# k2's projection by Strassen's algorithm, the output projection's first row tile in two groups, weight sums in place

## The chip, the cores and the metric

The kernel runs on one core of a Trainium2 chip, as one launch. Its metric is the device time of an execution in microseconds (us). TensorE (PE) multiplies matrices; VectorE (DVE) and ScalarE (ACT) work on tiles element by element; GpSimd (POOL) and SyncE (SP) here mostly issue DMAs. Each engine runs its instructions in order and waits on semaphores for the others. SBUF is the on-chip memory of 128 partitions; PSUM, in banks of 512 float32 per partition, takes the results of matmuls.

## The reference

A layer of a graph network with a feed-forward block, all in float32. x has N = 384 rows (nodes) of F = 1024 features.

```python
h = layernorm(x)
q, k, v = h @ wq.T + bq, h @ wk.T + bk, h @ wv.T + bv
q2, k2, v2 = q @ wiq.T + biq, k @ wik.T + bik, v @ wiv.T + biv     # then 16 heads of 64
mask = full((N, N), -inf); mask[src, dst] = softplus(w)[type - 1]   # 12288 edges, the last one wins
mask[i, i] = w[3] where it is still -inf
attn = softmax(q2 @ k2.T / 8 + mask)                                # for each head
x = x + (attn @ v2) @ wo.T + bo
y = layernorm(x)
g = silu(y @ w1.T * s1) * (y @ w2.T * s2)
x = x + gelu(gelu(g @ h1.T * t1) @ h2.T * t2) @ w3.T * s3
```

The seven matrices w* of the attention are 1024 x 1024; those of the feed-forward block are ternary.

## The kernel before, in words

**Layout.** Activations are kept transposed, features on partitions in 8 blocks of 128 and the 384 nodes along the row; v2 and the output projection have nodes on partitions, in three row tiles. A weight matrix is loaded as two halves of 512 output columns, 2 MB each, into a pool of four buffers (`load_w`, `prefetch`). `plan` names the halves in the order of their use; a half is asked for when an earlier one is done with. All these loads go through SP's queue; only the feed-forward weights, rounded on the way, go through POOL's.

**Order.** The instructions of SP, ACT, DVE and PE stand in the order in which the program writes them; POOL's are placed by the scheduler, with the DMAs of `load_w` kept in program order. The stages on PE: transposes of the normalised x, q (`project`), q2, v (`project_fast`), v2, k (`project_fast`), then k2 with the attention, the output projection, the feed-forward block (`rest`).

**Strassen's algorithm (Winograd's form).** `project_fast` computes a 1024 x 1024 projection by seven products of half the size. Its operands are sums of quarters of the input (`row_sums`: s1 to s4) and of quarters of the weight (b11 to b22). A product is 16 matmuls of 128 x 128 weights with 192 columns, into two of six PSUM banks; DVE and ACT add the products up. The weight sums are DVE operations on 128 x 2048 elements: `third` writes b22 - b12 into a tile t3 of its own, `first` makes b12 - b11 in place of b12, then b11 += t3 and b21 -= b11 stand between the products (lines 459 to 501). The functions in `beside` are called between the products: chunks of the edge table, weight sums for the next stage, or the bias `xs += bo`. v2 does the same with nodes on partitions, for two of its three row tiles (lines 531 to 571); the third is multiplied directly (`last_tile`).

**The mask.** The 12288 edges, 96 columns of 128, are scattered into a table in DRAM by 96 indirect DMAs on POOL, one column each. Where a cell occurs twice the last edge has to win: `targets` compares, on DVE, each edge with those of the next columns, and sends the earlier ones to a spare cell. `flight` is how many columns may be under way at once: 3 for those groups of 16 columns that `DENSE` lists, else 2. A `chunk` is eight columns. The values and the fill are negated, since the softmax works on -score: `nmask` is read back (line 575, on POOL) once the last scatters have landed, and the k2 projection carries the factor -0.125.

**The attention.** There are 24 units: a pair of heads and a row tile of 128 nodes. They run in 13 slots of mostly two units. In a slot PE multiplies the scores (`scores`, in PSUM tiles of a pool of four), DVE adds the mask and takes the row's extreme (`exponentials`), ACT makes the exponentials and their sums, DVE scales them (`normalised`); in the next slot PE transposes them (`transposed`) and DVE and ACT copy the results to SBUF; when three units of a pair are there, `weighted` multiplies with v2, and ACT adds the bias into aT. Between the two units' transposes PE does matmuls of the k2 projection. `project_k2` is a generator of 64 matmuls, 8 for each of 8 output blocks of 128 features: AHEAD = 3 blocks go ahead of the first slot, the others are shared out over the slots. Its results and the products av take turns in a pool of two PSUM banks. In the last two slots and after them PE begins the output projection (`out_steps`, eight matmuls of 512 columns for a row tile and half). `inspect` reads the feed-forward weights once to see whether they are exact in a short format: SP loads 512 KB, ACT reduces them.

**The end.** `multiply_out` and `add_out` finish the output projection and its sum with x row tile by row tile, each followed by its layernorm; the feed-forward block begins with rows 0 to 255 while row tile 2 is normalised. The last outputs are multiplied, added and stored one after the other.

## Time and profile before

| | |
|---|---|
| Median of three runs | 402.02 us (400.39 to 405.31) |
| Profiled execution | 396.56 us, of which 394.3 us are the profile's span |
| PE busy | 383.2 us (97%) |
| DVE, POOL, ACT busy | 234.1, 129.7, 106.1 us |
| TensorE clock granted | 0.996 |
| DMA | 59.88 MB, mean 152 GB/s |

Stages on PE, by the chain that ended last (us from the span's start): first matmul of q 13.2; q2 54.5 to 92.1; v to 128.6; v2 to 166.4; k to 202.8; k2's first three blocks to 218.3; the slots to about 299.6; the output projection to 340.7; the feed-forward block to 382.2; the last additions to 390.6.

A line of the page names the line of the kernel, the engine and the operation, then the tile written and those read, the shape and the count; behind the bar stand the busy time in us and the mean of one in ns, and then how long the engine had stood idle before these instructions and what ended that. In a timeline each row is a start, a duration, and in brackets an idle time just before it and its releaser. Consecutive instructions on an engine overlap a little, so the distance from start to start is the better price. Waits give a total, how often, and the longest.

### The profile page before, as it was taken

To read this page: it belongs to the slowest core of one execution; us is meant where nothing else is said; L and a number is where in the kernel's file an instruction comes from. 1 tells how busy PE (TensorE), PEld (TensorE's weight loads), DVE (VectorE), ACT (ScalarE), POOL (GpSimd) and SP (SyncE) were. 2 spreads that over 40 slices of the span, in tenths; PEclk is the share of its full clock that TensorE was granted. 3 is DMA by queue.
4 is the path that set the end of the run, shared out by engine and by line. 5 is a ranking of instruction groups with operands and counts; after the bars stand their busy time and mean duration, and the time that the engine had idled before them with its cause. 6 is when DMAs were issued, how large, how long until landed. Compare 5 with 4: busy or idle time off the path is not lost.

```text
span 394.3 us, 4956 instructions
## 1 busy us (share of the span) xinstructions
PE 383.2 (97%) x1829; PEld 277.8 (70%) x1829; DVE 234.1 (59%) x623; ACT 106.1 (27%) x235; POOL 129.7 (33%) x114
## 2 busy tenths in 40 slices
PE   6899999999999999999999999999999999999994
PEld 6555578999999444599985556564645445699983
DVE  5695798974699773653720396767751055222456
ACT  3610010000000010020001287757761386142420
POOL 3024466785686287777742000000000000200000
PEclk9999999999999999999999999999999999999998
DMA  8799998319320920380086281011196040570004
GB/s 284 244 363 310 292 302 303 92 48 378 112 68 19 364 99 0 118 309 2 0 278 256 61 265 57 12 42 53 32 342 216 0 161 0 143 284 0 2 1 163
DMA packets 30250, 59.88 MB, mean 152 GB/s; under 512 B 5424, under 2 KB 8336, under 8 KB 30096
## 3 DMA queue, kind: packets, MB, share of 16 engines
q1 hardware_dynamic: 23056, 50.09, 37.0%
q0 software_dynamic: 6880, 9.03, 7.9%
q10 hardware_dynamic: 288, 0.41, 0.3%
q8 instruction: 16, 0.26, 0.3%
q14 instruction: 10, 0.08, 0.1%
HBM read 57.26 MB, written 2.26 MB: 151 GB/s over the span
## 4 chain that ended last, share of the span: by engine, by line
PE 79%; DVE 11%; DMA 8%; ACT 1%; issue 0%; SPq 0%; DVEq 0%; ACTq 0%
PE ps L454 25%; PE ps L598 11%; PE ps L619 10%; PE ps L538 10%; PE ps L800 6%; DMA wiq<-in_wiq 5%; PE av L676 4%; PE sc L635 4%; PE pp L667 4%; PE ps L812 4%; DVE jk L350 3%; DMA xs<-in_x 1%; DVE y L895 1%; DMA kr<-keyd 1%; DVE y L894 1%; DVE sums L415 1%
## 5 line engine op out<-in xcount | busy, mean ns | idle before, releaser
L366 POOL DMA_INDIRECT tab<-val,cell x96 | 121.3, 1263 | 90.8 <-DMA tab<-val,cell 43.9
L350 DVE SCALAR_TENSOR_TENSOR jk<-kr,key,jp 128x384 bf16<-128x384 f32 (+1 forms) x96 | 48.2, 564 | 5.4 <-DMA kr<-keyd 5.4
L619 PE MATMUL ps<-kT,wik 128*128 128x384 f32 x128 | 43.4, 487 | 0.0
L598 PE MATMUL ps<-wo,aT 128*128 128x512 f32 x96 | 42.6, 594 | 0.0
L152 PE MATMUL ps<-xT,wq 128*128 128x384 f32 x128 | 41.5, 487 | 0.3 <-ACT xT L266 0.3
L152 PEld LDWEIGHTS ps<-xT,wq 128*128 128x128 f32 x128 | 24.2, 190 | 17.2 <-ACT xT L266 0.5
L649 DVE CUSTOM_DVE_ANT_0 e<-sc,nmask 128x384 f32<-128x384 f32 x48 | 23.9, 552 | 19.3 <-DMA nmask<-tab 18.9
L619 PEld LDWEIGHTS ps<-kT,wik 128*128 128x128 f32 x128 | 23.4, 190 | 14.4 <-ACT k2T L622 0.5
L651 ACT ACTIVATE e<-e,lo 128x384 f32<-128x384 f32 x48 | 28.9, 604 | 12.3 <-DVE lo L649 12.0
L598 PEld LDWEIGHTS ps<-wo,aT 128*128 128x128 f32 x96 | 17.7, 190 | 20.2 <-issue 20.2
L800 PE MATMUL ps<-x,w 128*128 128x384 f32 (+2 forms) x176 | 25.8, 306 | 0.0
L800 PEld LDWEIGHTS ps<-x,w 128*128 128x128 f32 x176 | 25.1, 190 | 0.5 <-issue 0.5
L667 PEld LDWEIGHTS pp<-ident,e 128*128 128x128 f32 x144 | 16.2, 140 | 12.0 <-issue 6.2
L538 PE MATMUL ps<-wiv,vT 128*128 128x512 f32 x56 | 24.5, 592 | 0.0
L101 POOL DMA_DIRECT2D w<-in_w x3 | 2.6, 859 | 64.8 <-DVE e L659 56.1
L667 PE MATMUL pp<-ident,e 128*128 128x128 f32 x144 | 20.6, 278 | 0.3 <-ACT pTb L707 0.3
L538 PEld LDWEIGHTS ps<-wiv,vT 128*128 128x128 f32 x56 | 10.6, 190 | 12.9 <-issue 12.2
L101 POOL DMA_DIRECT2D h<-in_h x2 | 1.5, 762 | 54.0 <-issue 54.0
L635 PE MATMUL sc<-k2T,q2T 64*128 64x384 f32 x96 | 19.0, 511 | 0.0
L659 DVE TENSOR_SCALAR e<-e,rd 128x384 f32<-128x384 f32 x48 | 18.0, 417 | 0.9
L193 ACT ACTIVATE junk<-raw 128x1024 bf16<-128x1024 uint16 x16 | 16.9, 1056 | 0.2
L622 ACT ACTIVATE k2T<-ps,biks 128x384 f32<-128x384 f32 x8 | 4.6, 580 | 45.6 <-PE ps L619 45.6
(162 smaller groups left out, 578.5 us busy)
## 6 DMA issues: line engine op xcount, KB each, us to landing
kr<-keyd SPq DMA_DIRECT2D x11, 640.0 KB, 5.2
raw<-in_w SPq DMA_DIRECT2D x12, 512.0 KB, 4.9
w<-in_w POOLq DMA_DIRECT2D x3, 2048.0 KB, 12.3
wiq<-in_wiq SPq DMA_DIRECT2D x2, 2048.0 KB, 18.2
wv<-in_wv SPq DMA_DIRECT2D x2, 2048.0 KB, 12.7
wiv<-in_wiv SPq DMA_DIRECT2D x2, 2048.0 KB, 7.7
wk<-in_wk SPq DMA_DIRECT2D x2, 2048.0 KB, 11.3
wik<-in_wik SPq DMA_DIRECT2D x2, 2048.0 KB, 8.5
```

Of the source, the lines that this page charges most:

```text
L152: nc.tensor.matmul(ps[:, :N], lhsT=w[:, k, o * P:(o + 1) * P], rhs=src[:, k, :], start=(k == 0), stop=(k == nk - 1))
L350: nc.vector.scalar_tensor_tensor(jk[:, :w], krf[:, j * P:j * P + w], key[:, c:c + 1], later[:, :w], op0=ALU.is_equal, op1=ALU.mult, accum_ ...
L366: i = nc.gpsimd.indirect_dma_start(out=tab, in_=val[:, c:c + 1], in_offset=None, out_offset=bass.IndirectOffsetOnAxis(ap=cell[:, c:c + 1], ...
L454: nc.tensor.matmul(ps[o // 2][:, o % 2, :HN], lhsT=w[:, k, o * P:(o + 1) * P], rhs=x[:, k, :], start=(o % 2, k) == (0, 0), stop=(o % 2, k) ...
L538: nc.tensor.matmul(ps, lhsT=x, rhs=w, start=i == 0, stop=i == len(steps) - 1)
L598: nc.tensor.matmul(ps, lhsT=aT[:, k, t * P:(t + 1) * P], rhs=wos[half][:, k, :], start=k == 0, stop=k == KF - 1)
L619: nc.tensor.matmul(ps[:, :N], lhsT=wik[o // 4][:, k, o % 4 * P:(o % 4 + 1) * P], rhs=kT[:, k, :], start=k == inputs[0], stop=k == inputs[-1])
L635: nc.tensor.matmul(sc[:, :N], lhsT=q2T[r, pair, t * P:(t + 1) * P], rhs=k2T[r, pair, :], start=True, stop=True)
L649: nc.vector.tensor_tensor_reduce(e, sc[:, :N], nmask[:, t, :], 1.0, 3e38, op0=ALU.add, op1=ALU.min, accum_out=lo)
L651: nc.scalar.activation(e, e, AF.Exp, bias=lo, scale=-1.0, accum_out=dens[u][:, j:j + 1])
L667: nc.tensor.transpose(pt[:, m, :], e[:, m * P:(m + 1) * P], ident)
L800: nc.tensor.matmul(ps[:, rows], lhsT=w[:, k, o * P:(o + 1) * P], rhs=x[:, k, rows], start=n == 0, stop=n == len(todo) - 1)
```

## The change

- **k2** becomes Strassen's algorithm as well, in three pieces: output features 0 to 511 as one (seven products of eight matmuls), ahead of the first slot; features 512 to 767 and 768 to 1023 as one each (seven products of four matmuls), in the slots 0 to 8. Quarters are taken by pairs of blocks (`paired`). Sums and uses are written into the order as a product is finished: at once in the first piece, after the third matmul of the next product, or at the start of the next slot, in the other two (`waiting`, `flush`). The row sums s1, s2, s4 are new tiles in the attention's pool; a21 - a11 is made in place.
- The score carries no factor any more: the mask's values are multiplied by 8, not negated, and the first softmax step multiplies by -0.125 (`w8`, `mask`; the bias tile `biks` goes).
- **Weight sums in place:** `third` writes b22 - b12 into b12; after the product that uses it, b12 becomes b22 - b11. t3 and its pool go, and the calls in `beside` are moved accordingly.
- **wo** is loaded through POOL's queue, behind the mask's reading.
- **The output projection's row tile 0** is made in two groups of four matmuls each: the first four blocks of features in slots 9 and 10, added to x at once; the others from slot 11 on. Row tile 1 is begun after the slots. The end is reordered so that `transpose_x2` of row tiles 0 and 1 both stand within row tile 2.
- Eight inspections lie in the slots instead of six; columns 80 to 95 may have three scatters under way (`DENSE` gets 5); the feed-forward block's staging tiles get a pool of their own.

```diff
-DENSE = (0, 1, 2, 4)
-AHEAD = 3
+DENSE = (0, 1, 2, 4, 5)
...
-            queue = nc.gpsimd if rounded else nc.sync
+            queue = nc.gpsimd if rounded or late else nc.sync
...
-            queue.append(load_w(*plan.pop(0), between=between))
+            name, parts = plan.pop(0)
+            queue.append(load_w(name, parts, late=name[:2] == "wo", between=between))
...
         def third(at=0):
             b11, b12, b21, b22 = blocks(at)
-            t3 = tp.tile([P, HK, FH], FP, tag="t3", name="t3")
-            minus(t3, b22, b12)
-            return t3
-        def first():
-            b11, b12, b21, b22 = blocks()
-            minus(b12, b12, b11)
+            minus(b12, b22, b12)
+        def paired(w, g):
+            w = w.rearrange("p k (g h c) -> p k g h c", h=2, c=P)[:, :, g]
+            return [w[:, k:k + HK, :, h] for k in (0, HK) for h in (0, 1)]
+        def paired_third(w):
+            b11, b12, b21, b22 = paired(w, slice(0, 2))
+            minus(b12, b22, b12)
...
             beside[0]()
-            m7 = product(t3, s3)
-            nc.vector.tensor_add(b11, b11, t3)
+            m7 = product(b12, s3)
+            nc.vector.tensor_add(b11, b11, b12)
             beside[1]()
+            minus(b12, b22, b11)
             m6 = product(b11, s2)
...
-            t3 = third()
-            first()
+            third()
             chunk()
             sums_q = row_sums(qT, HN, tag="v2")
-            t3s = []
-            project_fast(qT, sums_q, t3, q2T, vec[:, BIQ:],
-                         [chunk, chunk, chunk, lambda: t3s.append(third(2))])
+            project_fast(qT, sums_q, q2T, vec[:, BIQ:],
+                         [nothing, lambda: (chunk(), chunk()), chunk, lambda: third(2)])
...
-            project_fast(xT, sums_x, t3, kT, vec[:, BK:], [first, *(biased(t) for t in range(NT))])
+            project_fast(xT, sums_x, kT, vec[:, BK:], [biased(t) for t in range(NT)] + [lambda: paired_third(queue[2][0])])
...
-        def project_k2():
-            for o in range(KF):
-                ps = ps_mm.tile([P, 512], FP, tag="mm", name="ps")
-                for k in inputs:
-                    nc.tensor.matmul(ps[:, :N], lhsT=wik[o // 4][:, k, o % 4 * P:(o % 4 + 1) * P],
-                                     rhs=kT[:, k, :], start=k == inputs[0], stop=k == inputs[-1])
...
+        s1, s2, s4 = (ap.tile([P, HK, HN], FP, name=f"s{i}") for i in (1, 2, 4))
+        a11, a12, a21, a22 = quarters(kT, HN)
+        waiting = []
+        def flush():
+            while waiting:
+                waiting.pop()()
+        def project_k2(half, g, lag):
+            b11, b12, b21, b22 = paired(wik[half], g)
+            c = k2T[:, 4 * half:4 * half + 4, :].rearrange("p (g h) n -> p g h n", h=2)[:, g]
+            c11, c12, c21, c22 = (c[:, :, h, r:r + HN] for r in (0, HN) for h in (0, 1))
+            n = g.stop - g.start
+            def copies(ps):
+                nc.scalar.copy(c11, ps)
+                nc.scalar.copy(c12, ps)
+                nc.vector.tensor_add(b11, b11, b12)
...
+            for w, x, use in ((b11, a11, copies), (b21, a12, m2),
+                              (b11, s2, lambda ps: nc.vector.tensor_add(c12, ps, c12)),
+                              (b12, a21, m7), (b21, a22, lambda ps: finish(c21, ps, c22, 0)),
+                              (b12, s1, m5), (b22, s4, lambda ps: finish(c12, ps, c12, 1))):
+                ps = ps_mm.tile([P, 2, 256], FP, tag="mm", name="ps")
+                for i in range(n):
+                    for k in range(HK):
+                        nc.tensor.matmul(ps[:, i, :HN], lhsT=w[:, k, i, :], rhs=x[:, k, :],
+                                         start=(i, k) == (0, 0), stop=(i, k) == (n - 1, HK - 1))
+                        if i * HK + k == lag - 1:
+                            flush()
+                        yield
+                waiting.append(lambda ps=ps[:, :n, :HN], use=use: use(ps))
+                if lag == 0:
+                    flush()
...
-        k2 = project_k2()
-        done, pairs, left = 0, 0, (KF - AHEAD) * KF
-        for _ in range(AHEAD * KF):
-            next(k2)
+        nc.vector.tensor_add(s1, a21, a22)
+        minus(s2, s1, a11)
+        for step, _ in enumerate(project_k2(0, slice(0, 2), 0)):
+            if step == 2 * HK:
+                minus(a21, a11, a21)
+                minus(s4, a12, s2)
+        paired_third(wik[1])
+        k2 = chain(*(project_k2(1, slice(g, g + 1), 3) for g in range(2)))
+        steps, done, pairs = 2 * 7 * HK, 0, 0
...
-                    share = min(7 + -(-(left - 7) * s // (len(slots) - 3)), left) - done
+                    share = min(10 + -(-(steps - 10) * s // 8), steps) - done
...
+                    if s in (9, 10):
+                        ps = ps_mm.tile([P, 512], FP, tag="mm", name="ps")
+                        out_steps(ps, 0, s - 9, 0, HK, HK)
+                        half = slice((s - 9) * FH, (s - 8) * FH)
+                        nc.vector.tensor_add(xs[:, 0, half], ps, xs[:, 0, half])
+                    elif s == 11:
+                        begin(0, 0, HK, HK + 2)
+                        begin(0, 1, HK, HK + 1)
+                    elif s == 12:
+                        begin(0, 0, HK + 2, KF - 1)
+                        begin(0, 1, HK + 1, KF - 1)
-            if s in (1, 3, 5, 7, 9, 10):
+            if s in (1, 2, 3, 4, 5, 7, 9, 10):
                 inspect_more(False, 1)
```

## The prediction

> **What bounds the kernel now.** First the page: TensorE (PE) is busy for 97% of the span, so only a stretch in which it stands still, or work taken off it, can move the end.
>
> ```profile
> span 394.3 us, 4956 instructions
> PE 383.2 (97%) x1829; PEld 277.8 (70%) x1829; DVE 234.1 (59%) x623; ACT 106.1 (27%) x235; POOL 129.7 (33%) x114
> ```
>
> Then the waits of PE alone (us in total, times, longest): after its start it stands still for 1.2 us, all in two places.
>
> ```profile
> PE ps L454 <- DVE wiq L483: 0.9, 1, 0.9
> PE pp L667 <- ACT pTb L707: 0.3, 1, 0.3
> ```
>
> Then the groups, for the price of a matmul. Each float32 matmul leaves two records.
>
> ```profile
> L619 PE MATMUL ps<-kT,wik 128*128 128x384 f32 x128 | 43.4, 487 | 0.0
> L454 PE MATMUL ps<-xT,wk 128*128 128x192 f32 x96 | 16.1, 326 | 0.0
> ```
>
> Records overlap, so I price by spacing: 24 matmuls of 384 columns from 202.80 to 218.28 are 0.645 each; the chain's 192 matmuls of 192 columns in 62.67 us are 0.326 each. Half the columns cost half.
>
> Last the timelines where two DMA chains come near PE: POOL with the scatter's end, DVE with the first softmax step, PE with the first transposes of attention.
>
> ```profile
> 197.99 0.96 POOL L366 DMA_INDIRECT tab<-val,cell  x1 [0.30 <-issue]
> 199.27 0.96 POOL L366 DMA_INDIRECT tab<-val,cell  x1 [0.33 <-DMA tab<-val,cell]
> 204.23 0.96 POOL L366 DMA_INDIRECT tab<-val,cell  x1 [4.00 <-DMA tab<-val,cell]
> ...
> 215.21 0.96 POOL L366 DMA_INDIRECT tab<-val,cell  x1 [2.09 <-DMA tab<-val,cell]
> 217.97 0.80 POOL L575 DMA_DIRECT2D nmask<-tab  x1 [1.80 <-DMA tab<-val,cell]
> ```
>
> ```profile
> 222.47 0.56 DVE L649 CUSTOM_DVE_ANT_0 e<-sc,nmask 128x384 f32<-128x384 f32 x1 [18.89 <-DMA nmask<-tab]
> ...
> 224.66 0.75 DVE L659 TENSOR_SCALAR e<-e,rd 128x384 f32<-128x384 f32 x2
> ```
>
> ```profile
> 225.26 0.87 PE L667 MATMUL pp<-ident,e 128*128 128x128 f32 x6
> ```
>
> The normalised tile is finished at 225.32, PE transposes it from 225.26: this profile has no PE wait there, and nothing to spare either. A later mask would have moved the end one for one.
>
> **What the Trainium skill says.** "Trainium Kernel Development and Optimization", Key Constraints: DMAs from SP, ACT and POOL run on the same 16 engines and interleave. The trace agrees: wo is issued at 197.6 from SP, and scatters from POOL, 1.27 apart before, then wait 4.00 and 4.44. "DMA: Bandwidth & Descriptors", Anatomy of one DMA — SWDGE: a fixed cost of about 2 us, mostly the receipt; here the scatters land 2.1 us after issue at best, 3.7 in the median. "Perfetto Trace Analysis", Identifying the Most-Contended Engine: matmul busy time is a poor measure, weight-load busy a good one. In the 192-column stage from 92 to 128.5 us weight loads are busy 36.5 of 36.5, so a 192-column matmul is at its floor and nothing can be hidden below it.
>
> **The change part by part**, against the profiled execution (396.56 us, span 394.3; the median of the runs is 402.02, 5.5 more).
>
> *k2 by Strassen.* 64 x 0.645 = 41.3 becomes 7 x 16 = 112 matmuls x 0.326 = 36.5: **-4.8**. It is all PE work, so all of it counts unless PE then waits.
>
> *Weight sums in place.* Each projection still has four 2.3 us weight sums, now in another order. In q2's, the old order put two sums, two chunks of targets (4.7 each) and the row sums ahead of `b11 += t3`, which ended at 65.92, and PE waited 0.9. Now one sum (45.9 to 48.2), one chunk (to 52.9) and the row sums (from qT at 55.3 to 59.0) stand ahead, and the new `b11 += b12` runs once m1 has been read, 59.7 to 62.0; m6 needs it at 65.0. **-0.9**. The two chunks behind it end near 71, then the second difference, by 73.5; m5 needs that at 75.3, and PSUM bank 0 of m7 free at 75.0. So cover is 0.3 to 1.8 us there; gone, a late kr (it came at 66.97) costs its lateness. In v, v2 and k the same walk leaves over 1 us each: nothing. POOL's issues run 25 us and more behind the chunks: nothing. k2 can start at 202.8 - 0.9 = 201.9.
>
> *First half of k2.* In the built program its first row sum, s1 on DVE, waits for all 96 scatters to land: its tile lies where the scatter's index tiles were. This wait is new; behind it on DVE stand s2, `b11 += b12` and all later uses, and PE's third product waits for them. When does the scatter end? Column 90 went at 199.27; without wo's traffic five more at 1.27 come to 205.6; a third one in flight for columns 80 to 95 takes away the waits above 0.30 there, about -0.7; from last issue to landing 217.9 - 215.2 = 2.7: **207.6**. Bounds: 205 (all landings at 2.1, no POOL hold-up) and 212 (the first two raw loads, 1 MB together and formerly behind wo, now go right after wik near 167 and meet the scatter; one 4.4 us wait like that at 210.9). Then 0.88 + 0.97 for s1, s2 (rows of 768 elements) and 1.13 for the sum of 1024 (half of 2.28): 210.6. PE is there at 201.9 + 16 x 0.326 = 207.1: **+3.5**, one for one with the scatter's end above 204.1. Five products later, each sum one product ahead, the half ends at 201.9 + 18.3 + 3.5 = 223.7. The mask, read at 208, is there by 213 (4.5 as before): no longer last.
>
> *Second half, in the slots.* I laid every slot out by hand in the built order, counting from 223.7, with spacings of this trace: DVE 0.48 an exponential's row step, 0.48 a copy, 0.86 a normalisation, 0.64 a 512-element sum, 0.33 a 192-column use; ACT 0.60 an exponential, 0.40 a copy, 1.11 an inspection; PE 1.49 for four scores, 1.47 for two transposes, 2.09 for av. DVE gets 3 sums and 7 uses per quarter, 4.2 us, twice. PE stalls:
> - slot 0, third product: uses 0.7, difference 1.13, first softmax 2.85 (222.47 to 225.32) and b11's sum 0.64 end at 5.3; PE is there after 0.85 + 8 x 0.326 = 3.5: 1.9.
> - slot 2, sixth product: the b12 difference stands behind four exponentials, a copy and a normalisation: 1.3.
> - slot 4, second product needs the bank of the seventh, whose use is behind a normalisation: 1.0.
> - slot 5, av needs a bank that ACT frees by two copies behind an inspection: 0.6.
> - slot 7, no av to give time: the second transposes wait for ACT's copy behind four exponentials, as at 284.5 before: 0.8.
>
> Together **+5.6**, of which the 0.3 of before goes away: **-0.3**. Bounds 2.5 (DVE and ACT each 10% ahead of my walk) and 8 (each slot without av adds a further 1).
>
> *wo's first row tile in two groups.* The same 48 matmuls of 0.86; 14 instead of 6 lie in slots. Two more DVE additions of 0.69 fall in slots 9 and 10, where DVE needs 5.3 of over 6.4 us: nothing, 1.4 if that cover were gone. The tail keeps its order of latencies, and four banks suffice.
>
> *Queues.* wo's two issues of some 0.9 go on POOL behind the mask read; they wait for wk's last use at 201.9, which is past. They need 10 to 20 us and are used near 284: nothing. w1 behind them is used after 340. Two more inspections in slots 2 and 4 are in my ACT times. The mask's new sign and scale is the same instruction.
>
> Sum: -4.8 - 0.9 - 0.3 + 3.5 + 5.6 = +3.1; 396.56 becomes 399.7. The runs lie 5.5 above the profile. Nothing here shows why; the zero-slack scatter is the likeliest carrier, and of its waits the part under wo goes and the rest stays and still counts one for one. I carry a third, 1.8: **401.5**.
>
> **The rivals.** *The scatter does not gate.* For: POOL could run at 1.27 to the end without wo, 205. Against: 27 of its 96 issues waited for a landing. The end is then 396.56 - 6.0 + 0.9 (gate at 205) + 3.5 (slots in the lower half) = 395, and the runs' excess goes with wo's traffic. *The scatter gates harder.* The wait that took the mask's place lies 15 us earlier in PE's work, and the inspection loads are pulled into the scatter. With its end at 213 the stall is 8.9, not 3.5: 405.1, and with the same 1.8 and another 1 of slots 408. It makes the kernel slower than before from an end of 208.1 on, since the forecast at 207.6 is 0.5 under the median. *The change does not do what it says:* no gain from halved columns. Against it the 0.326; 404 if so.
>
> **How the numbers follow.** Forecast 401.5, between 398 and 405: 0.48. No gate, 395: 0.32. Harder gate, 408: 0.17. No gain: 0.03. A measurement tells about 2% from no change, 394.0 and 410.1. Of the second case less than half lies below 394, 0.14; of the third half above 410, 0.09; within 0.77. Range 393.5 to 408, which leaves out 0.12 below and 0.09 above.
>
> **What would show it.** The waits of PE: about 3.5 us for DVE's b11 sum near 207 to 211, 1.9 in the first slot, none at q2's m6. DVE's idle before the first mask step is gone and stands before s1 instead, ended by the scatter. The last scatter at 205; PE busy near 378; k2's matmuls 326 ns. Wrong if the scatter ends by 204 or after 211, if the slots stall under 3, or if the runs' excess sits elsewhere.

## The result, and the profile after

The changed kernel takes 404.55 us, the median of 20 runs (402.92 to 409.58). In the same comparison the kernel before takes 403.27 us, also over 20 runs (397.36 to 412.95). The ratio is 1.0136, with a 95% interval of 1.0091 to 1.0182; it compares only the runs within 1.5% of the fastest of their kernel, 19 of the changed kernel's 20 and 10 of the other's, while the medians over all runs lie 1.3 us, or 0.3%, apart. By the ratio the change is slower by a small amount that the measurement can tell from nothing. The prediction was 401.5 us and no change. Its range held the time; its direction did not.

Chips differ in how far the runs of one kernel spread, so below only kernels that ran together on one chip are compared by their medians.

The profiled execution took 408.77 us. Its page begins:

```profile
span 406.7 us, 5195 instructions
...
PE 385.8 (95%) x1925; PEld 294.0 (72%) x1925; DVE 258.7 (64%) x664; ACT 103.4 (25%) x233; POOL 126.4 (31%) x116
```

Strassen was to lower PE's busy time of 383.2 us to about 378. It rose instead, and the span grew by 12.4 us. The waits of PE (us in total, how often, the longest) show part of it:

```profile
PE ps L457 <- issue: 5.1, 8, 1.1
...
PE ps L671 <- DVE wik L644: 1.9, 1, 1.9
PE ps L671 <- DVE wik L414: 1.7, 1, 1.7
PE ps L671 <- DVE k2T L649: 1.1, 1, 1.1
...
PE av L730 <- ACT k2T L643: 0.6, 1, 0.6
PE pp L721 <- ACT pTb L766: 0.5, 1, 0.5
...
PE pp L721 <- DVE pTb L765: 0.2, 1, 0.2
```

The six lower ones are the slot stalls that the prediction listed, each in its place: 1.9 (1.9 predicted), 1.7 (1.3), 1.1 (1.0), 0.6 (0.6), and 0.7 (0.8) for the second transposes of slot 7. The wait of 0.9 in q2 is gone. The first line is new: PE idle for eight short times, with nothing that the profile sees it wait for. They are not in k2, which the change rewrites, but in k before it. The groups of PE (busy us and mean ns of one, then the idle time before):

```profile
L671 PE MATMUL ps<-kT,wik 128*128 128x192 f32 x128 | 22.8, 328 | 1.1 <-DVE k2T L649 1.1
...
L457 PE MATMUL ps<-xT,wk 128*128 128x192 f32 x96 | 21.2, 374 | 4.7 <-issue 4.6
```

k2's matmuls of 192 columns take 328 ns, as priced. k's, the same instruction as before, went from 326 to 374 ns. By windows of the span (sum; busy us and records of PE, PEld, DVE, ACT, POOL; granted clock, DMA share, GB/s) the place is plain:

```profile
196.00:200.00 4.00, 2.27 (x11) 1.29 (x10) 3.03 (x6) 0.00 (x0) 3.02 (x4) 1.00 0.02 0
200.00:204.00 4.00, 1.77 (x7) 1.27 (x6) 0.00 (x0) 0.00 (x0) 3.08 (x4) 0.71 0.02 0
204.00:208.00 4.00, 2.75 (x8) 2.08 (x8) 1.20 (x4) 0.00 (x0) 2.19 (x3) 0.50 0.08 7
208.00:212.00 4.00, 4.00 (x15) 4.00 (x14) 0.84 (x3) 0.00 (x0) 0.17 (x1) 0.51 0.95 319
```

First PE's records become few at full clock, then the granted clock falls to a half. The last product of k started at 197.08 and k2 only at 212.15, where 5.2 us lie between them in an undisturbed stage. That is 9.9 us lost. I call it PE's **standing still** below, though group 2 shows that other engines have a part in it.

It also hides the scatter's gate. POOL's timeline (start, duration, idle before and its releaser), then DVE's and PE's at the places that the prediction showed:

```profile
203.65 0.96 POOL L366 DMA_INDIRECT tab<-val,cell  x1 [0.30 <-issue]
206.42 0.80 POOL L575 DMA_DIRECT2D mask<-tab  x1 [1.81 <-DMA tab<-val,cell]
```

```profile
212.35 0.74 DVE L477 SCALAR_TENSOR_TENSOR kT<-ps,vec,kT 128x192 f32<-128x192 f32 x2 [3.51 <-PE ps L457]
213.13 0.96 DVE L744 TENSOR_TENSOR s<-kT 128x768 f32<-128x768 f32 x1
...
232.35 0.55 DVE L703 CUSTOM_DVE_ANT_0 e<-sc,mask 128x384 f32<-128x384 f32 x1
...
234.53 0.75 DVE L713 TENSOR_SCALAR e<-e,rd 128x384 f32<-128x384 f32 x2
```

```profile
238.34 0.87 PE L721 MATMUL pp<-ident,e 128*128 128x128 f32 x6
```

The scatter has landed by 206.4 (predicted 207.6). With PE late, the row sum s1 starts at 213.13 without waiting for it. DVE's 18.89 us of idle before the first mask step are gone, as said.

So three questions went to the chip. Does the standing still belong to the change? Do the predicted terms hold where it is absent? And what do they then leave over?

### The profile page after: what moved, and what is told of

Read it like the earlier page. It is cut to its first block, busy times and chain, and to the rows that moved or that the text cites. A ratio compares the mean times of both kernels' runs of the same rounds, so it can differ in the third digit from the quotient of the medians.

```text
span 406.7 us, 5195 instructions
## 1 busy us (share of the span) xinstructions
PE 385.8 (95%) x1925; PEld 294.0 (72%) x1925; DVE 258.7 (64%) x664; ACT 103.4 (25%) x233; POOL 126.4 (31%) x116
## 4 chain that ended last, share of the span: by engine, by line
PE 86%; DVE 8%; ACT 2%; issue 2%; DMA 1%; SPq 0%; ACTq 0%
PE ps L457 28%; PE ps L601 10%; PE ps L151 10%; PE ps L538 9%; PE ps L671 7%; PE ps L870 6%; PE av L730 4%; PE ps L882 4%; PE pp L721 3%; PE sc L689 3%; DVE e L703 2%; DVE e L713 1%; DMA xs<-in_x 1%; DVE y L965 1%; DVE y L964 1%
## 5 line engine op out<-in xcount | busy, mean ns | idle before, releaser
L366 POOL DMA_INDIRECT tab<-val,cell x96 | 116.2, 1210 | 84.3 <-DMA tab<-val,cell 32.2
L457 PE MATMUL ps<-xT,wk 128*128 128x192 f32 x96 | 21.2, 374 | 4.7 <-issue 4.6
L870 PEld LDWEIGHTS ps<-x,w 128*128 128x128 f32 x176 | 25.1, 190 | 0.5 <-issue 0.5
L703 DVE CUSTOM_DVE_ANT_0 e<-sc,mask 128x384 f32<-128x384 f32 x48 | 23.9, 553 | 1.0 <-PE sc L689 1.0
L457 PEld LDWEIGHTS ps<-xT,wk 128*128 128x128 f32 x96 | 19.0, 222 | 7.1 <-issue 7.0
L671 PE MATMUL ps<-kT,wik 128*128 128x192 f32 x128 | 22.8, 328 | 1.1 <-DVE k2T L649 1.1
L671 PEld LDWEIGHTS ps<-kT,wik 128*128 128x128 f32 x128 | 20.7, 190 | 2.2 <-DVE k2T L649 2.0
L457 PE MATMUL ps<-sums,wk 128*128 128x192 f32 x128 | 21.5, 327 | 0.5 <-issue 0.5
L457 PEld LDWEIGHTS ps<-sums,wk 128*128 128x128 f32 x128 | 20.9, 190 | 0.9 <-issue 0.7
L457 PE MATMUL ps<-sums,wiq 128*128 128x192 f32 x128 | 21.1, 326 | 0.0
L457 PE MATMUL ps<-sums,wv 128*128 128x192 f32 x128 | 21.1, 326 | 0.0
```

What stands on the lines that cost most here:

```text
L366: i = nc.gpsimd.indirect_dma_start(out=tab, in_=val[:, c:c + 1], in_offset=None, out_offset=bass.IndirectOffsetOnAxis(ap=cell[:, c:c + 1], ...
L457: nc.tensor.matmul(ps[o // 2][:, o % 2, :HN], lhsT=w[:, k, o * P:(o + 1) * P], rhs=x[:, k, :], start=(o % 2, k) == (0, 0), stop=(o % 2, k) ...
L671: nc.tensor.matmul(ps[:, i, :HN], lhsT=w[:, k, i, :], rhs=x[:, k, :], start=(i, k) == (0, 0), stop=(i, k) == (n - 1, HK - 1))
L703: nc.vector.tensor_tensor_reduce(e, sc[:, :N], mask[:, t, :], -0.125, 3e38, op0=ALU.add, op1=ALU.min, accum_out=lo)
L870: nc.tensor.matmul(ps[:, rows], lhsT=w[:, k, o * P:(o + 1) * P], rhs=x[:, k, rows], start=n == 0, stop=n == len(todo) - 1)
```

## The experiments

They ran in five groups. The kernels of one group ran on one chip, together with the kernel before. Medians and lowest times are over all runs; ratios are to before in the same group, formed as above.

| Group | Kernel | Median us (lowest) | Ratio, 95% interval |
|---|---|---|---|
| 1 | before | 406.58 (397.0) | |
| 1 | e1 changed | 406.96 (406.51) | 1.0233 [1.0164, 1.0302] |
| 1 | e2 sums moved | 405.79 (403.09) | 1.0201 [1.0122, 1.0280] |
| 1 | e3 wo through SP | 410.28 (409.02) | 1.0306 [1.0238, 1.0374] |
| 1 | e4 half Strassen | 399.65 (392.92) | 0.9978 [0.9921, 1.0036] |
| 2 | before | 401.48 (396.41) | |
| 2 | x2 without Strassen | 404.49 (403.17) | 1.0141 [1.0075, 1.0207] |
| 2 | x3 second half only | 409.78 (408.49) | 1.0273 [1.0210, 1.0335] |
| 2 | x4 other sharing | 404.64 (398.38) | 1.0082 [1.0036, 1.0128] |
| 3 | before | 396.82 (395.98) | |
| 3 | y1 half Strassen, wo through SP | 393.19 (392.80) | 0.9918 [0.9905, 0.9932] |
| 3 | y2 sums moved, wo through SP | 397.93 (397.68) | 1.0045 [1.0025, 1.0065] |
| 3 | y3 without Strassen, wo through SP | 395.25 (394.69) | 0.9965 [0.9953, 0.9977] |
| 3 | y4 half Strassen, with small transfers | 393.14 (393.01) | 0.9912 [0.9899, 0.9924] |
| 4 | before | 397.84 (395.85) | |
| 4 | z1 changed | 403.91 (401.36) | 1.0155 [1.0108, 1.0201] |
| 4 | z2 changed, with small transfers | 406.20 (403.84) | 1.0227 [1.0180, 1.0275] |
| 4 | z3 half Strassen | 393.38 (393.32) | 0.9888 [0.9845, 0.9930] |
| 4 | z4 half Strassen, wo through SP | 393.34 (392.79) | 0.9894 [0.9850, 0.9939] |
| 5 | before | 402.39 (397.41) | |
| 5 | w1 sums moved | 404.88 (403.29) | 1.0127 [1.0065, 1.0190] |
| 5 | w2 changed | 406.60 (405.40) | 1.0168 [1.0107, 1.0230] |

### Group 1: the gate, wo's place, and half of Strassen

*e1* is the changed kernel once more.

> The changed kernel once more, for a second trace. Scatter theory: the slow clock between 196 and 212 us of the first trace belongs to that execution; here the last product of k takes 5.2 us as the others do, then the first row sum s1 stands waiting for the scatters (end 205 to 209), and PE waits 2.5 to 5 us for DVE's b11 sum at the third product of k2; span about 401. Clock theory: the change itself lowers the clock in the projection of k, and the last product of k is again stretched by about 10 us.

*e2* moves the row sums into the buffer of v2's sums, so that s1 doesn't stand where the scatter's index tiles were.

```diff
-        pTs = [act.tile([P, KF, N], FP, tag="t", name="pTa", bufs=2),
-               ap.tile([P, 2 * NT, N], FP, name="pTb")]
+        pTs = [ap.tile([P, 2 * NT, N], FP, name=f"pT{i}") for i in "ab"]
...
-        s1, s2, s4 = (ap.tile([P, HK, HN], FP, name=f"s{i}") for i in (1, 2, 4))
+        sums = act.tile([P, 4, HK, HN], FP, tag="t", name="sums", bufs=2)
+        s1, s2, s4 = (sums[:, i] for i in range(3))
```

> s1, s2, s4 lie in a buffer that no scatter tile used; the second transposed tile takes their place in the attention's pool. Nothing else is changed. Scatter theory: s1 no longer waits for a DMA, the third product of k2 starts without a wait, and the time falls by the length of that wait, 2.5 to 5 us, to 399 to 401. Rival (the slots alone cost, or the clock): no change, 403 to 404.

*e3* loads wo through SP's queue again.

```diff
-            queue.append(load_w(name, parts, late=name[:2] == "wo", between=between))
+            queue.append(load_w(name, parts, between=between))
```

> The changed kernel with wo loaded through SP's queue again. Scatter theory: the wo load meets the last scatters, which end 9 to 11 us later (216 to 218), and the third product of k2 waits that much longer: plus 8 to 11 us, 411 to 415. Rival (the place of the wo load does not matter, since the mask has slack): 403 to 405.

*e4* is e2 with the second half of k2 as 32 plain matmuls of 384 columns in the slots; the difference a11 - a21 gets a tile of its own, since a21 is still read.

```diff
-        paired_third(wik[1])
-        k2 = chain(*(project_k2(1, slice(g, g + 1), 3) for g in range(2)))
-        steps, done, pairs = 2 * 7 * HK, 0, 0
+        k2 = plain_k2()
+        steps, done, pairs = 4 * KF, 0, 0
...
-                    share = min(10 + -(-(steps - 10) * s // 8), steps) - done
+                    share = min(6 + -(-(steps - 6) * s // 8), steps) - done
```

> As the run with the sums moved, and the second half of k2 is again multiplied directly in the slots (32 matmuls of 384 columns, no additions on DVE). Slot theory: the five PE stalls in slots 0 to 7, 6.0 us, go, and 32 x 0.645 - 56 x 0.326 = 2.4 us of matmuls come back: 3.6 under the run with the sums moved, 395.5 to 397.5. Rival (those stalls are hidden by something later): 2.4 over that run.

Measured: e3 shows the gate in full. Its timelines of DVE, of PE and of POOL:

```profile
213.71 0.96 DVE L744 TENSOR_TENSOR s<-kT 128x768 f32<-128x768 f32 x1 [11.38 <-DMA tab<-val,cell]
```

```profile
217.00 4.91 PE L671 MATMUL ps<-s,wik 128*128 128x192 f32 x16 [10.32 <-DVE wik L644]
```

```profile
209.06 0.96 POOL L366 DMA_INDIRECT tab<-val,cell  x1 [2.95 <-DMA tab<-val,cell]
214.22 0.80 POOL L575 DMA_DIRECT2D mask<-tab  x1 [4.19 <-DMA tab<-val,cell]
```

Beside wo's 4 MB the scatter lands at 213.7 instead of 206.4, s1 starts at that moment, and PE's third product 3.3 us later. The new wait that the prediction found in the built program is real. The median is 3.3 us above e1's (410.28 against 406.96), just under the range expected; since e1's profile has the standing still and e3's has not, that is not the price of wo's place alone.

In e2 the wait for the scatter is gone, but the median fell by only 1.2, not by 2.5 to 5. The profiles of e1 and e2 have PE's standing still again, at 205 to 212 and at 197 to 207, so e1 was not the 401 us expected either. e4's profile has none, and its lowest, 392.92, is 4.1 below before's lowest; the prediction's terms give -3.9 (-2.4 for half of k2, -1.2, -0.3). Its median, 399.65, is above the range expected and 1.7% below before's, but its ratio, 0.9978, can't be told from 1. Half of Strassen keeps half of the gain and has no slot stalls at all: after the start PE waits for nothing.

### Group 2: does the standing still belong to the change?

*x1* is the kernel before itself, profiled a second time.

> The kernel before once more, for a second look into where its time goes when it is not at its lowest. Theory A (PE's standing still at 196 to 212 us, for which nothing in the profile of the changed kernel gives a cause, is no part of the change; it comes to any of these kernels): a span above 396 us has PE idle put down to issue, or a granted clock below 0.99, somewhere in 190 to 230 us. Theory B (it comes from the longer stretch of 192-column matmuls that the first half of k2 adds): no such idle time in 190 to 230 us, clock 0.99 or more, and whatever lies above 396 us is a wait for the mask before the first transposes of the attention.

*x2* is the changed kernel with before's k2: 64 plain matmuls, 24 of them ahead of the slots; they read the blocks of k in plain order, where before read the second half of the blocks first.

```diff
-        for step, _ in enumerate(project_k2(0, slice(0, 2), 0)):
-            if step == 2 * HK:
-                minus(a21, a11, a21)
-                minus(s4, a12, s2)
-        paired_third(wik[1])
-        k2 = chain(*(project_k2(1, slice(g, g + 1), 3) for g in range(2)))
-        steps, done, pairs = 2 * 7 * HK, 0, 0
+        k2 = plain_k2(range(KF))
+        for _ in range(3 * KF):
+            next(k2)
+        steps, done, pairs = 5 * KF, 0, 0
```

> The changed kernel with the k2 projection of before (64 matmuls of 384 columns, 24 of them ahead of the first slot); all else as changed: weight sums in place, wo behind the mask, first row tile in two groups, the fifth DENSE group. By the prediction's terms: -1.2 (q2's wait and the start of k), -0.3; lowest 397.0 - 1.5 = 395.5 us, and the slots without a wait of PE. Theory A: median 3 to 6 above its lowest, as with the others. Theory B: no stretch of PE idle put down to issue, clock 0.99 or more, median within 3 of the lowest.

*x3* is the reverse of e4: the first half plain, the second by Strassen's algorithm in the slots.

```diff
-        for step, _ in enumerate(project_k2(0, slice(0, 2), 0)):
-            if step == 2 * HK:
-                minus(a21, a11, a21)
-                minus(s4, a12, s2)
+        minus(s3, a11, a21)
+        minus(s4, a12, s2)
+        for _ in plain_k2(range(HK)):
+            pass
```

> The first half of k2 by 32 plain matmuls of 384 columns ahead of the slots, the second half by Strassen's algorithm in the slots as in the changed kernel; row sums in the buffer of v2's sums, so that no sum waits for the scatter; all else as changed. By the terms: -2.4 (32 x 0.645 less 56 x 0.326), -1.2, +6.7 for the slots' stalls (the five waits as in the changed kernel: 1.9, 1.7, 1.1, 0.6, 0.5), -0.3: +2.8, lowest 397.0 + 2.8 = 399.8 us. Theory A: median 3 to 6 above. Theory B: no PE idle put down to issue, median within 3 of the lowest.

*x4* is e2 with the second half shared out otherwise.

```diff
-        steps, done, pairs = 2 * 7 * HK, 0, 0
+        for _ in range(2 * HK):
+            next(k2)
+        steps, done, pairs = 12 * HK, 0, 0
...
-                    share = min(10 + -(-(steps - 10) * s // 8), steps) - done
+                    share = min(8 + 5 * s, steps) - done
```

> The changed kernel with the row sums in the buffer of v2's sums (no sum behind the scatter) and with another sharing of the second half: its first two products ahead of the first slot, so that their uses stand ahead of the first softmax on DVE, then eight matmuls in slot 0 and five in each of slots 1 to 8. If the slots' stalls are what eats Strassen's gain, PE's waits there fall from 6.0 to 2 us or less, and the time lies 4 to 5 us below that of the kernel with the sums moved alone (403.1 lowest, 405.8 median): 398 to 399 lowest, 401 median. Theory A allows a run without PE's standing still: then 392 to 394. Theory B: PE idle put down to issue in 190 to 230 us again, in every run, none below 397. If the stalls only move to other slots: 403 and 406 again.

Measured: x1 settles the first question. It took 403.32 us, and its waits of PE and PE's timeline show the same thing in the unchanged kernel:

```profile
PE ps L454 <- issue: 3.8, 10, 0.6
...
PE ps L454 <- DVE wiq L483: 0.7, 1, 0.7
```

```profile
193.99 0.81 PE L454 MATMUL ps<-sums,wk 128*128 128x192 f32 x4 [0.25 <-issue]
195.44 1.08 PE L454 MATMUL ps<-sums,wk 128*128 128x192 f32 x4 [0.63 <-issue]
196.89 2.70 PE L454 MATMUL ps<-sums,wk 128*128 128x192 f32 x15 [0.38 <-issue]
```

k took 41.25 us here (from 167.90 to k2's first matmul at 209.15) instead of 36.4. Theory A holds: standing still comes to the kernel before too. In this run it is 4.9 of the 6.8 us above the 396.56 us of the profile that the prediction was built on; what the other runs of before carry, one profile can't say.

PE is not alone in it. In the changed kernel's first profile DVE adds up two products of k late, released by nothing that the profile shows ("remote"):

```profile
196.83 0.56 DVE L473 TENSOR_TENSOR kT<-ps,kT 128x384 f32<-128x384 f32 x1 [3.76 <-remote]
206.80 2.04 DVE L477 SCALAR_TENSOR_TENSOR kT<-ps,vec,kT 128x192 f32<-128x192 f32 x6 [6.95 <-remote]
```

PE had run without a gap up to 196.36, as it did in the undisturbed profile of group 4 (z1), where the first of these additions starts at 191.29: DVE was 5.5 us late before PE first stopped. In e1 the last product of k was finished when k2 began at 201.31, but DVE's last addition of it began at 208.58, and ACT copied k2's first product at 208.73 (201.69 and 204.29 in z1). POOL went on with the scatter, one issue every 1.27 us.

x2 and x3 have it as well, so their times can't be read as sums of terms, and both expectations by lowest time missed (403.17 for 395.5, 408.49 for 399.8). In x2 it is DVE that stands still: PE waits before k2 for 3.3 us, put down to issue, and for 2.8, put down to DVE, and goes on both times 0.47 us after DVE begins the addition of k that the next matmul reads, at 204.39 and 208.73, although PE's last product of k was over by 201.6. x3's slots nevertheless repeat the changed kernel's waits, but for the first, which is 1.0 and not 1.9: 1.0, 1.7, 1.1, 0.6, 0.5 and 0.2 us.

x4 was to take the slot stalls away. It moved them. Its waits of PE:

```profile
PE ps L671 <- DVE k2T L649: 1.9, 1, 1.9
...
PE ps L671 <- DVE rd L711: 1.6, 1, 1.6
...
PE pp L721 <- ACT pTb L768: 0.8, 2, 0.5
PE pp L721 <- DVE pTb L767: 0.5, 1, 0.5
PE ps L671 <- ACT aT L733: 0.3, 1, 0.3
```

That is 5.1 us in the slots where the changed kernel has 6.0. Products of four matmuls last 1.3 us, less than DVE and ACT need to get past a slot's exponentials, copies and normalisation (the first softmax alone is 2.85 us in the prediction's walk); this other order of the steps didn't help.

### Group 3: does the missing traffic bring it about?

In every profile with the standing still, no bulk transfer had run since about 177 us, and it was over about when the scatter ended and bulk transfers came back. wo behind the mask makes that quiet stretch longer. y1, y2 and y3 are e4, e2 and x2 with wo through SP's queue (the edit of e3). y4 is e4 with nine small transfers in the stretch:

```diff
+            scrap = dram.tile([P, P], FP, name="scrap")
+            def last_bias():
+                biased(2)()
+                for _ in range(9):
+                    nc.sync.dma_start(scrap, xs[:, 2, :P])
```

> The kernel with the first half of k2 by Strassen's algorithm and the second half plain (row sums not behind the scatter), and wo again through SP's queue, issued when wk is done with, near 197 us. Theory C (PE stands still, and everything on it slows, when no bulk transfer has run for some 15 us beside the scatter, and it ends when transfers return; so the changed kernel brought it about in nearly every run by holding wo back until after the mask): PE has no idle time put down to issue between 190 and 230 us, the clock is 0.995 or more, wo slows the scatter to an end near 215, the mask is there near 221, when the first slot needs it; lowest 393, median 394 to 397 us. Theory D (the standing still belongs to the scatter or to chance, whatever else is transferred): as with wo behind the mask, median 399 to 400.

> The changed kernel with the row sums in the buffer of v2's sums (no sum behind the scatter) and wo again through SP's queue. Theory C: no PE idle put down to issue in 190 to 230 us; what remains is the prediction's own sum without the gate, -1.2 - 4.8 + 6.7 - 0.3 on a lowest of before of 396.4 to 397.0: lowest 397, median 398 to 401. Theory D: as with the sums moved and wo behind the mask, lowest 403, median 405.8.

> The changed kernel with before's k2 projection (24 of 64 matmuls ahead of the slots) and wo again through SP's queue; what is left of the change is the weight sums in place, the fifth DENSE group, the two groups of the first row tile and the two further inspections. Theory C: -1.2 - 0.3, lowest 395.3, median 396 to 401 (before's own median, 401.5, less the runs in which wo came too late to keep PE from standing still). Theory D: median 404 as with wo behind the mask.

> The kernel with the first half of k2 by Strassen's algorithm and the second half plain, wo behind the mask, and nine small transfers of 64 KB (a part of x to a scrap place in DRAM, which nobody reads) one behind the other through SP's queue from the third bias addition on, near 187 us; each 2 to 2.5 us from issue to landing, so that they run until 206 to 209. Theory C: no PE idle put down to issue between 190 and 210 us, clock 0.995 or more, lowest 393, median 394 to 397. Theory D: median 399 to 400 as without them. A finer form of C, that only a large transfer counts: then as D.

Measured: none of the four stands still, and their times come out close to the sums of terms: y3 1.6 us below before (1.5 expected), y1 3.6 below (3.9), y2 1.1 above (0.4, with the slots at the 6.7 that the expectations use for the prediction's 5.6). y1 and y2 differ in the second half of k2 alone. y2's median is 4.7 us longer, although its 56 matmuls at 0.326 are 2.4 us less work than y1's 32 at 0.645: Strassen's second half costs 7.1 us in the slots, with neither gate nor standing still in the profiles. But before's own runs all lay at 395.98 to 398.26 here, so the chip could be the reason as well as the traffic.

### Group 4: the traffic, or the chip?

*z1* is the changed kernel, *z2* the same with the small transfers of y4, *z3* is e4 and *z4* is y1.

> The changed kernel once more, beside the next one on one chip. Theory C (PE stands still and slows when beside the scatter no bulk transfer has run for some 15 us, until transfers return): PE idle put down to issue between 190 and 215 us as in its two profiles, median 403 to 408. Theory D (that comes with a chip or by chance, whatever is transferred): if before's runs all lie at 396 to 398 here, this one too is free of it, 400 to 401, which is before - 4.8 - 1.2 + 6.7 - 0.3 + 3 for the sum behind the scatter.

> The changed kernel with nine small transfers of 64 KB (a part of x to a scrap place in DRAM, which nobody reads) one behind the other through SP's queue from near 187 us on. Theory C: no PE idle put down to issue; the wait of the third product of k2 for the sum behind the scatter shows in full, 3 to 5 us (the scatter ends near 209 to 211 beside the transfers, 1 to 3 later than without); median 400 to 402, less than the changed kernel without them by 3 us or more. Theory D: the same time as the changed kernel, or longer by the scatter's delay.

> The kernel with the first half of k2 by Strassen's algorithm and the second half plain, row sums not behind the scatter, wo behind the mask, beside the next one on one chip. Theory C: PE's standing still in most runs, median 398 to 400. Theory D, on a chip where before's runs all lie at 396 to 398: 393.

> The same kernel with wo through SP's queue from near 197 us on. Theory C: 393, all runs within 1.5 us of it, on any chip; faster than before by 0.8% where before's runs are at their lowest, by more where they are not. Theory D: no difference from wo behind the mask.

Measured: theory C, that the quiet stretch is enough, falls. z3 has the long quiet stretch and takes 393.38 us, z4 doesn't have it and takes 393.34. On this chip no profile has PE idle put down to issue, with or without transfers; and on the chip of group 1 e4 had the quiet stretch, from 176.9 to 211.7, without standing still. z2 was not faster than z1 but 2.3 us slower. z1's median of 403.91 lies in the range that was given for C, but its profile has none of the idle time that C asks for.

z1's profile (401.36 us) is thus the changed kernel undisturbed, and the one to hold the prediction's sum against. Its waits of PE, PE's third product of k2 and the first of the three DVE sums ahead of it, which the scatter holds:

```profile
PE ps L671 <- DVE wik L644: 4.8, 2, 2.9
PE ps L671 <- DVE wik L414: 1.7, 1, 1.7
PE ps L671 <- DVE k2T L649: 1.1, 1, 1.1
```

```profile
209.79 2.84 PE L671 MATMUL ps<-s,wik 128*128 128x192 f32 x16 [2.94 <-DVE wik L644]
```

```profile
206.50 0.96 DVE L744 TENSOR_TENSOR s<-kT 128x768 f32<-128x768 f32 x1 [4.07 <-DMA tab<-val,cell]
```

The gate costs PE 2.9 us (the other 1.9 of the first line are slot 0's). But five of z1's six runs lie at 402.77 to 404.96 us, with a mean granted clock of 0.986 to 0.992 where the profiled one has 0.996. z2, with the same order and a gate of 3.9, shows where the clock can go (windows; the column before the last two is the granted clock):

```profile
204.00:208.00 4.00, 2.75 (x17) 2.45 (x16) 0.65 (x1) 0.86 (x2) 1.89 (x3) 1.00 0.02 0
208.00:212.00 4.00, 1.36 (x6) 1.39 (x7) 3.96 (x5) 0.00 (x0) 2.48 (x3) 0.89 0.66 189
212.00:216.00 4.00, 4.00 (x19) 4.00 (x18) 2.52 (x5) 0.00 (x0) 0.00 (x0) 0.69 1.02 386
```

The wait ends at 210.64. By the trace's record of the clock PE runs at half clock from 211.09 to 214.50, and its third product takes 4.36 us from start to start where z1's takes 2.68: 1.7 us of work lost on top of the wait. In e3 the clock is halved for 10.24 us, but from 210.98 on, while PE still waits until 217.00; the third product takes 4.75 us, so 2.1 are lost. "TensorE: Matmul & The Clock Gate" of the Trainium skill says in Part 1 that a window of some 3.4 us with PE idle brings the clock to a half. The traces agree with it in the length: the half-clock stretches inside the spans last 3.41, 6.83 or 10.24 us. They don't agree that PE has to be idle so long. In e1 a stretch of 3.41 us begins at 234.46, behind slot 0's wait of 1.9 us (231.20 to 233.07), although PE works on both sides of that wait; the same wait in the other profiles, and z1's gate of 2.9 us, have none behind them.

Which wait halved the clock in z1's other five runs is therefore not shown. y2 has the slots' waits and no gate, and three of its eight runs have a clock of 0.990 to 0.992 and take 399.04 to 400.45 us, the others 0.994 or more and 397.68 to 397.93.

### Group 5: what the gate costs beside the standing still

*w1* is e2, *w2* the changed kernel, on one chip.

> The changed kernel with the row sums in the buffer of v2's sums, so that no sum stands behind the scatter; wo behind the mask as changed; beside the next one on one chip. If the wait behind the scatter and what PE's halved clock takes after it are what lies between the sum of the terms and the time: third product of k2 waits under 1 us, clock 0.995, time as with wo through SP's queue on a chip where before's runs lie at 396 to 398: 397.7 to 398.5. If something else in the changed kernel costs it: within 1 us of the next one.

> The changed kernel, beside the one with the sums moved. Expected 3 us above it for the wait alone, and 1.7 us more (half of one stretch of 3.41 us at half clock) in those runs in which the granted clock over the span is 0.992 or less: 401 to 404 where the one with the sums moved has 398.

Measured: 404.88 and 406.60, 1.7 us apart, not 3 to 4.7, and both above their ranges. Both profiles have PE's standing still (2.8 and 5.9 us put down to issue), and in w2 it covers the gate as in the first profile of the changed kernel. On such a chip the gate is therefore partly free. On a chip without standing still its price is seen only within z1 and z2; e2 was not run there.

## Why the prediction was wrong

**The sum of the terms was 1.7 too low.** By z1, the profile that has neither standing still nor a halved clock in it, the changed kernel takes 401.36 us where the profile before took 396.56: +4.8, predicted +3.1. The two profiles were not taken side by side; on z1's own chip the changed kernel's lowest run is 5.5 above before's, and its median 6.1.

| Term | Predicted | Measured, z1 against before |
|---|---|---|
| k2 by Strassen | -4.8 | -4.8 (112 at 0.326, k2's spacing in the trace) |
| weight sums in place | -0.9 | -1.15 (k2 starts at 201.49, not 202.64) |
| sum behind the scatter | +3.5 | +3.1 (third product at 209.79, due at 206.7) |
| slots, with the 0.3 of before | +5.3 | +7.2 |
| start of the feed-forward block | +3.1 | +4.4 (344.56, not 340.12) |
| after it, and outside the span | 0 | +0.4 |

The step that failed is the **slots**: their stalls, put at +5.6, cost 7.1 to 7.5. The walk through them found every stall in its place, and the waits that the profile shows add up to 6.0. But the slots as a stage cost more. From the first scores to the last av they take 98.86 us; 56 matmuls at 0.326 and eight more wo matmuls at 0.86 explain 25.1 of it, 73.7 remain, and before the same rest was 66.5: 7.2 more, or 7.5 with the 0.3 of before. y2 against y1 gives 7.1. What the rest beside the waits consists of was not taken apart. Counted from start to start, PE loses 0.1 to 0.25 more at a wait than the wait says, and k2's matmuls stand in more and smaller groups. Here the sum of the waits was a lower bound of what a stalled stage loses. This term alone turns the forecast round: 401.5 and the missing 1.5 to 1.9 are 403.0 to 403.4, above the 402.02 of before.

**The clock had no term in the sum.** I counted PE's waits one for one. Behind the gate the clock was halved in z2 and e3, for 1.7 and 2.1 us more, and behind slot 0's wait in e1. In the first comparison 16 of the changed kernel's 20 runs have a mean clock of 0.992 or less and take 404.19 us or more; the other four have 0.995 or more and take 402.92 to 403.45. Which wait or gap halved it in those runs is not shown. After its start the profile before had no wait on PE's path above 0.9 us, so nothing there showed it.

**What the runs lie above the profile was carried wrongly.** I carried a third, 1.8 of 5.5 us, and named the scatter with no slack to spare as the likeliest carrier. x1 shows another one: PE and DVE stand still in k, in the kernel before, with DMA nearly silent. The change doesn't touch k's matmuls, so there was no reason to take two thirds of it away. In the comparison the changed kernel's median lies 3.2 above z1's 401.36, and it never fell under 402.92, while the kernel before fell to 397.36. With 4.8 for 3.1 and 3.2 for 1.8, the 401.5 becomes 404.55; that is bookkeeping, for the 3.2 is what the first number leaves over.

**The rivals.** That the scatter doesn't gate is refuted by e3 and z1. The harder gate was to need a scatter that ends after 208.1; it ended at 206.4 and 206.5, and the kernel was slower all the same, through the slots and, in many runs, the clock and the standing still. The upper part of the range was made for a late scatter, so that it held the time is luck. That halved columns gain nothing is refuted by the 328 ns.

**Costs put at nothing.** wo's two groups and the queue of wo: y3, which has the two groups and the weight sums in place, is 1.6 below before, so neither of these costs anything that shows. z3 against z4 finds no difference between the two queues where no sum stands behind the scatter. The thin cover at q2's m5, of which the prediction warned, was used up once: w2's profile has a PE wait of 1.0 us there.

**What stays open** is what makes PE and DVE stand still. It is in profiles of before, of the changed kernel and of most variants, in the first comparison and on three chips, and in no profile on two others; e3 and e4 were free of it on a chip that had it. It lies in the last 20 us of the scatter or just behind it, when hardly anything else is transferred; small transfers were tried only on chips that didn't show it without them.

## What to carry to other kernels

Where a matmul count falls by an eighth, ask how long one of its products is beside the work that DVE and ACT must do between two of them: k2's first half in products of eight matmuls kept its gain, the second half in products of four, among the softmax steps, lost more than it gained. Products of eight among those steps were not tried. The best version that the runs show is the first half alone (z3): 393.38 us, 0.9888 of before, with the row sums in a buffer that no DMA still reads; on the chip of group 1, with standing still, its gain could not be told from nothing (e4). And don't price a wait on PE of some 2 us or more as the wait alone: in these runs it cost up to 2 us more where the clock was halved behind it, which came in some executions and not in others.

## What was not expected of the hardware

- PE stands still for 0.2 to 1.8 us at a time with nothing to wait for, for a stretch of some 10 us in all, and DVE is held up in the same stretch: 3.8 us in ten gaps of PE in the kernel before (x1), 5.1 in eight gaps in the changed one, none in either group 3 or 4.
- Its aftermath can be almost as large: in the changed kernel's profile the clock was halved from 201.67 to 211.91, among and behind these gaps, so that 9.9 us were lost where 5.1 were idle. x1 had its gaps without a halved clock.
- The price of a wait that the prediction did expect: a tile placed where index tiles of indirect DMAs were made DVE wait for the last of 96 DMAs, 4.07 us in z1, and 11.38 in e3 with 4 MB of weights beside them. In y2, with the tile elsewhere, DVE did not wait.
